# A Perceiver layer on one core: query shifts by DMA, masks and divisions of the causal part regrouped, projections in column groups

## The chip, the cores and the metric

The kernel runs on 1 core of one Trainium2 chip. The metric is the device time of one execution in microseconds; the median of three runs of the kernel before is 1228.5 us (1228.21 to 1228.61).

The engines have the profiler's names: PE (TensorE) multiplies matrices, and PEld is the loading of its stationary operand; DVE (VectorE), ACT (ScalarE) and POOL (GpSimd) do the elementwise work; SP (SyncE) issues most DMAs. ACT and POOL can issue DMAs too, each in its own queue of instructions.

## The reference

The input x has B=4 sequences of T=256 rows with D=256 columns, and a context has 4096 rows for each sequence. Three residual steps follow one another; LN is a layer norm without weights:

```python
x = x + cross_attention(LN(x), ctx)    # 16 heads of 16; softmax over 4096 keys
x = x + causal(LN(x))                  # linear attention with random features
x = x + ffn(LN(x))                     # w_down(silu(w_gate h) * (w_up h)), hidden 768
```

In the cross-attention, Q = LN(x) Wq + bq, K = ctx Wk + bk, V = ctx Wv + bv, scores are QK/4, and the result goes through Wh + bh.

In the causal part, q and k of each head (16 numbers) are normalised to length 1 and turned into 64 features, `exp(clip(q·omega*sqrt(2s) - s, -20, 20))` times a weight, for two values of s and 32 columns of omega each. With features F(q), F(k), row t of the result is the sum over t' ≤ t of (F(q_t)·F(k_t')) v_t', divided by the same sum without v, at least 1e-6; then Wout + bout.

The weights of the feed-forward are int32 and are multiplied by 1/127.

## The kernel before

**Cross-attention** is the main loop. A unit u is one sequence b and one quad q of four heads (16 units). Each unit takes NS=16 steps of 256 keys. Row groups of 32 partitions hold the four heads of a quad: 16 rows of a head's numbers, one row (the first, 32j) for a shift, the rest zero or one. kts are three buffers of keys in that form, with ones in row 32j; so what stands in row 32j of the query tile qa is added to every score. It holds minus the maximum of that query's scores over all keys, which makes the exp safe.

Therefore the maxima of a unit must be known before its scores begin. In step n the loop computes, beside the scores of step n, the maxima of step s = n + NS + LEAD, with LEAD = 2: two steps before a unit ends, all the maxima of the next are there. At this point (w = 14) `shift` (L719 to L733) makes qa for it.

What PE, ACT and DVE do in one iteration n, in the order of their queues (`manual_schedule`: the order in which the code issues the instructions is the order in each queue of PE, ACT, DVE and SP; POOL's instructions are not in it):
- for heads (0,1), then heads (2,3): pt, the scores in row groups (L745), with pm, products for the maxima of the other two heads (L708); ACT takes e = exp(pt) (L750); DVE reduces pm to mx (L715).
- half of a projection of the context, for a later pair of units (EARLY = 8): pk (L642), which ACT copies as ku with the bias (L650) and SP's DMAs then put into kts (L653); or pv (L672), which ACT copies into v (L679). Both are in column groups: four matmuls of 32 columns each, side by side.
- pav (L765), values of step n−1, also in column groups, added by DVE to av (L775).
- at w = 14, `shift`: DVE reduces mx to neg, negated (L722), which is a sparse tile [128 queries, 2, 4, 32] of which only one column in 32 is not zero; after the projection's copy on ACT, `turn` (L724 to L731) transposes it on PE into pn (L727, two of 128*128), and DVE adds qT (L731), which gives qa. The call of `shift` is ahead of the projection in the code, that of `turn` behind its copy.
- at fixed steps of the next unit, `finish`: transposes pt_x, division, a bias on POOL (L802), eight small DMAs on SP (xo<-on, L806), transposes px, and the projection py (L823).

PSUM is one pool of 8 banks, taken in turn: a new tile waits until the readers of the tile that had the bank eight allocations before are done.

**The causal part** begins in the last two units: `start_causal` (L286 to L367) fills places of missing projections with pieces. In them `queries_keys` (L207, pqk of L211) and `values` (L224, pv1 of L229) project LN(x) with full 128*128 matmuls.

**The tail** begins near 1070 us, with a loop over n = 0 to 16 (L513 to L566). n is a sequence and quad of the causal part. At each n: values (po, L430; ACT copies it to avT, L435) of n−1; scores (pa, L411 and L416) of n, in two parts of two heads, each head's `at` multiplied by a mask on DVE (L421); `divide` of n−1 (PE transposes pt_o L442, DVE den L444 and L445, att L446); features of a later quad for some n (pf L275, DVE clip L281, ACT exp L282, POOL fac L283); then pieces of `fills[n]`: casts of the weights (ACT, L394, `weight(i)`, a whole weight of 768 KB each), output projection (L453), and the feed-forward of sequences that are done (L469). A weight is loaded when the one before has been cast.

The mask is made once on POOL by affine_select (L375): ones, and zeros where the key comes after the query, in the first and third of three blocks; the second block (first keys, second queries) needs none.

Of the kernel before, what the change touches and what calls it, by code (L numbers as in the profile page):

```python
# [20 lines left out]
P = 128  # L21
# [18 lines left out]
def perceiver_layer(  # L40
# [96 lines left out]
    def normalised(z, tiles):  # L137
# [47 lines left out]
    def causal_in(b):  # L185

        tiles = (2 * b, 2 * b + 1)
        z = lnp.tile([P, 2, D], F32, tag="z1", name="z1", bufs=4)
        got = []

        def norm():
            normalised(lambda t: z[:, t % 2, :], tiles)
            for t in tiles:
                nc.gpsimd.tensor_tensor(xr[:, t, :], xr[:, t, :], rest[9], ALU.add)

        def turn():
# [6 lines left out]
            nc.vector.tensor_copy(zT.rearrange("p k (i t) -> p k i t", t=P), ps)  # L203

        sqs = {}

        def queries_keys(i):  # L207
            t, zT = tiles[i], got[0]
            ps = bank([P, 2 * D], "pqk")
            for k in range(KC):  # L210
                nc.tensor.matmul(  # L211
                    ps, lhsT=zT[:, k, i * P : (i + 1) * P], rhs=rest[3][:, k, : 2 * D],
                    start=k == 0, stop=k == KC - 1,
                )
            nc.vector.tensor_tensor(qk[t], ps, rest[4][:, : 2 * D], ALU.add)
            sqs[i] = lnp.tile([P, 2 * D], F32, tag="sq", name="sq")
            nc.gpsimd.tensor_tensor(sqs[i], qk[t], qk[t], ALU.mult)

        def squares(i):
            nc.vector.tensor_reduce(  # L220
                nrm[:, tiles[i], :], sqs[i].rearrange("p (h d) -> p h d", d=HD), AX.X, ALU.add
            )

        def values():  # L224
            zT = got[0]
            ps = bank([P, 2, D], "pv1")
            for i in range(2):
                for k in range(KC):
                    nc.tensor.matmul(  # L229
                        ps[:, i, :], lhsT=zT[:, k, i * P : (i + 1) * P], rhs=rest[3][:, k, 2 * D :],  # L230
                        start=k == 0, stop=k == KC - 1,
                    )
# [52 lines left out]
    def start_causal():  # L285
# [75 lines left out]
        return norms, [call(lambda pieces: [piece() for piece in pieces], pieces) for pieces in others]  # L361

    finish = cross_attention(
        tc, xr, load_x, load_rest, ctxT, wq_sb, bq_sb, wkP, bk_sb, wvP, eps, ident, layernorm, transposed,
        qT, kts, lnp, bank, rest, start_causal)
    wout_sb = rest[8]

# [19 lines left out]
    coming = []  # L387

    def weight_load(i):
        src = (w_gate, w_up, w_down)[i]  # L390
        coming.append(load(src, list(ws[i].shape), "w_i", mybir.dt.int32, nc.sync, late))

    def weight(i):
        nc.scalar.activation(ws[i], coming[i], AF.Copy, scale=(1.0, 0.5, 1.0)[i] / 127.0)  # L394
        if i + 1 < len(ws):
            weight_load(i + 1)

    def attend(n):


        b, q = divmod(n, NQ)
        ats, got = [], []

        def scores():
            for part in range(2):
# [12 lines left out]
                    )  # L418
                for pa in pas:
                    at = work.tile([P, 3, P], F32, tag="at", name="at", bufs=8)  # L420
                    nc.vector.tensor_tensor(at, pa, mask, ALU.mult)  # L421
                    ats.append(at)

        def values():
            po = bank([P, T], "po")
            for i in range(2):
                for j, at in enumerate(ats):
# [6 lines left out]
            oT = work.tile([P, T], F32, tag="avT", name="avT")  # L434
            nc.scalar.copy(oT, po)  # L435
            got.append(oT)

        def divide():
            oT = got.pop()
            pt = bank([P, 2, 4, 32], "pt_o")  # L440
            for i in range(2):
                nc.tensor.transpose(pt[:, i].rearrange("p j r -> p (j r)"), oT[:, i * P : (i + 1) * P], ident)  # L442
            den = work.tile([P, 2, 4], F32, tag="den", name="den")
            nc.vector.tensor_scalar(den, pt[:, :, :, HD], 1e-6, None, ALU.max)  # L444
            nc.vector.reciprocal(den, den)  # L445
            nc.vector.tensor_tensor(  # L446
                att[:, 2 * b : 2 * b + 2, 64 * q : 64 * q + 64].rearrange("p t (j d) -> p t j d", d=HD),
                pt[:, :, :, :HD], den.unsqueeze(3).to_broadcast([P, 2, 4, HD]), ALU.mult,
            )

        return scores, values, divide
# [61 lines left out]
    with tc.manual_schedule(engines={ET.PE, ET.Activation, ET.DVE, ET.SP}):  # L513
        normalise, turn15, project15 = finish
        normalise()
        weight_load(0)
# [3 lines left out]
        fills[1] += [lambda: weight(0)]  # L520
        fills[2] += [turn15, lambda: weight(1)]
        fills[3] += [project15, norm3, lambda: weight(2)]
# [45 lines left out]

def cross_attention(tc, xr, load_x, load_rest, ctxT, wq_sb, bq_sb, wkP, bk_sb, wvP, eps,
                    ident, layernorm, transposed, qT, kts, lnp, bank, rest, start_causal):  # L570

# [20 lines left out]
    with ExitStack() as st:  # L592
# [4 lines left out]

        vs = big.tile([P, NCH, KT, VP], F32, tag="v", name="v")

        negs = [big.tile([P, 2, 4, 32], F32, tag=f"neg{i}", name="neg") for i in range(2)]  # L600


        wk_sb = big.tile([P, KC, D], F32, tag="wk_sb", name="wk_sb")
# [26 lines left out]
        def key(p, c, queues=(nc.sync, nc.sync)):  # L630
# [5 lines left out]
            def half(part):  # L636
# [1 line left out]
                made.append(pk)  # L638
                cs = slice(part * (CH // 2), (part + 1) * (CH // 2))
                for k in range(KC):  # L640
                    for j in range(4):
                        nc.tensor.matmul(  # L642
                            pk[32 * j : 32 * j + 32, :],
                            lhsT=wk_sb[:, k, m * P + 32 * j : m * P + 32 * j + 32], rhs=x[:, k, cs],
                            start=k == 0, stop=k == KC - 1,
                        )

            def out(part):
                cs = slice(part * (CH // 2), (part + 1) * (CH // 2))
# [10 lines left out]
        def value(p, c):  # L660
# [4 lines left out]
            def half(part):  # L665
                pv = bank([P, 2, P], "pv")
                made.append(pv)
                for i in range(2):
                    t0 = (2 * part + i) * P
                    for k in range(KC):  # L670
                        for j in range(4):
                            nc.tensor.matmul(  # L672
                                pv[32 * j : 32 * j + 32, i, :], lhsT=x[:, k, t0 + 32 * j : t0 + 32 * j + 32],
                                rhs=wv_sb[:, k, m * P : (m + 1) * P], start=k == 0, stop=k == KC - 1,
                            )

            def out(part):
                to = vs[:, c, 2 * part : 2 * part + 2, : 8 * (HD + 1)]
# [38 lines left out]
            return products, reduce  # L717

        def shift(u):  # L719
            b, q = divmod(u, NQ)  # L720
            neg = negs[u % 2]
            nc.vector.tensor_reduce(neg[:, :, :, 0], mxs.pop(u), AX.X, ALU.max, negate=True)  # L722

            def turn():  # L724
                pn = bank([P, T], "pn")
                for i in range(2):
                    nc.tensor.transpose(  # L727
                        pn[:, i * P : (i + 1) * P], neg[:, i].rearrange("p j r -> p (j r)"), ident
                    )
                qas[u] = small.tile([P, T], F32, tag="qa", name="qa")  # L730
                nc.vector.tensor_tensor(qas[u], pn, qT[:, q, b * T : (b + 1) * T], ALU.add)  # L731

            return turn  # L733

# [42 lines left out]
        def finish(u):  # L777
# [41 lines left out]
            def project():  # L819
                t, oT = 2 * b + q // 2, rows_of.pop(b)  # L820
                py = bank([P, D], "py1")
                for k in range(KC):
                    nc.tensor.matmul(  # L823
                        py, lhsT=oT[:, k, :], rhs=rest[1][:, k, :], start=k == 0, stop=k == KC - 1
                    )
# [35 lines left out]
        with tc.manual_schedule(engines={ET.PE, ET.Activation, ET.DVE, ET.SP}):  # L861
# [33 lines left out]
            for neg in negs:  # L895
                nc.vector.memset(neg, 0.0)
            for piece in normal[1]:
                piece()
            whole(key(0, 2))
# [55 lines left out]
            for n in range(NU * NS + 1):  # L955
# [113 lines left out]
```

## Time and profile before

| | |
|---|---|
| median of three runs | 1228.5 us |
| the profiled execution's own time | 1229.02 us |
| its span | 1227.3 us |
| mean granted PE clock | 0.997 of full |
| DMA, mean over the span | 78 GB/s |
| PE over the 40 slices, in tenths | 7 in the first, 9 in the next 34, then 5, 9, 9, 9, 8 |

The span is cut into 40 slices of 30.7 us. PE's busy share is at 90% or more from the second slice to the 35th, between 50 and 60% in the 36th (1074 to 1105 us, the first stretch of the tail), and at 80% or more to the end. The main loop is thus the part from about 73 us, when unit 0's qa is there, to about 1068 us.

How much each kind of work costs, from the groups of instructions: busy time in us, mean of one in ns.

```profile
L715 DVE TENSOR_REDUCE mx<-pm 128x1 f32<-128x512 f32 x1024 | 635.6, 684 | 145.4 <-PE pm L708 145.3
L750 ACT ACTIVATE e<-pt 128x512 f32<-128x512 f32 x1024 | 529.2, 602 | 384.2 <-PE pm L708 359.6
L745 PE MATMUL pt<-qa,kt 32*128 32x256 f32 x4096 | 500.2, 388 | 1.3 <-DVE av L775 0.7
L708 PE MATMUL pm<-kt,qT 32*128 32x512 f32 x2048 | 494.6, 616 | 0.0
L765 PE MATMUL pav<-e,v 128*32 128x256 f32 x4096 | 269.8, 380 | 0.0
L672 PE MATMUL pv<-wv_sb,ctx 128*32 128x128 f32 x4096 | 137.5, 276 | 0.0
L642 PE MATMUL pk<-ctx,wk_sb 128*32 128x256 f32 x2048 | 136.7, 388 | 0.0
```

A line has: line of the program, engine, operation, output<-inputs, for PE the size of the stationary tile (32*128 is a row group of 32 partitions, 128*32 a column group), shapes, count; then busy time and mean; then the idle time of the engine just before such instructions and what ended most of it. Matmuls in different groups of the array overlap, so their means don't add up to PE's time.

### The profile page before, as it was taken

What the parts mean: (1) busy time and instruction counts of PE and PEld (TensorE: products, weight loads), DVE (VectorE), ACT (ScalarE), POOL (GpSimd) and SP (SyncE); (2) the same over time, 40 slices, a digit from 0 to 9 for tenths busy, and PEclk for the clock granted to TensorE, in tenths of its full rate; (3) what the DMA queues carried; (4) which work ended last, traced back from release to release, by engine and by line L of the source; (5) the groups of instructions that cost most, each with busy time, mean ns of one, the idle gap of its engine ahead of it and who ended that gap; (6) DMA issues with size and microseconds to landing.
All of it is one profiled execution on the core that took longest, in us unless ns stands there. A gap on an engine that the chain in (4) does not pass through costs nothing.

```text
span 1227.3 us, 42096 instructions
## 1 busy us (share of the span) xinstructions
PE 1193.0 (97%) x17712; PEld 807.0 (66%) x17712; DVE 927.9 (76%) x1823; ACT 673.0 (55%) x1394; POOL 60.2 (5%) x115
## 2 busy tenths in 40 slices
PE   7999999999999999999999999999999999959998
PEld 3566667666766676667666776677667755536777
DVE  6887777777777777777777777777788877577763
ACT  3456665566666655666656556655566546641311
POOL 4010000000000000000000000000001012120100
PEclk9999999999999999999999999999999999999999
DMA  6452331233123322332233213322232000020000
GB/s 208 135 192 67 101 114 56 80 105 106 64 79 89 116 71 63 103 119 72 60 102 106 86 58 91 103 90 73 86 105 91 5 1 4 2 80 1 10 9 18
DMA packets 57756, 95.78 MB, mean 78 GB/s; under 512 B 29024, under 2 KB 31712, under 8 KB 57568
## 3 DMA queue, kind: packets, MB, share of 16 engines
q1 hardware_dynamic: 56640, 92.44, 24.3%
q8 instruction: 140, 2.29, 0.8%
q10 hardware_dynamic: 416, 0.66, 0.2%
q14 instruction: 48, 0.39, 0.1%
q0 software_dynamic: 512, 0.00, 0.0%
HBM read 74.17 MB, written 1.05 MB: 61 GB/s over the span
## 4 chain that ended last, share of the span: by engine, by line
PE 92%; DVE 4%; ACT 1%; DMA 1%; issue 1%; SPq 0%; POOL 0%; DVEq 0%; ACTq 0%
PE pt L745 22%; PE pm L708 18%; PE pav L765 18%; PE pk L642 11%; PE pv L672 10%; PE pd L504 2%; PE pg L492 1%; PE pu L492 1%; PE pq L848 1%; PE pqk L211 1%; PE po L430 1%; PE pa L411 1%; PE py L823 1%; PE py L466 1%; DVE mx L715 1%; PE pf L275 1%
## 5 line engine op out<-in xcount | busy, mean ns | idle before, releaser
L715 DVE TENSOR_REDUCE mx<-pm 128x1 f32<-128x512 f32 x1024 | 635.6, 684 | 145.4 <-PE pm L708 145.3
L750 ACT ACTIVATE e<-pt 128x512 f32<-128x512 f32 x1024 | 529.2, 602 | 384.2 <-PE pm L708 359.6
L745 PE MATMUL pt<-qa,kt 32*128 32x256 f32 x4096 | 500.2, 388 | 1.3 <-DVE av L775 0.7
L708 PE MATMUL pm<-kt,qT 32*128 32x512 f32 x2048 | 494.6, 616 | 0.0
L745 PEld LDWEIGHTS pt<-qa,kt 32*128 32x128 f32 x4096 | 317.0, 184 | 117.2 <-ACT v L679 43.2
L765 PE MATMUL pav<-e,v 128*32 128x256 f32 x4096 | 269.8, 380 | 0.0
L708 PEld LDWEIGHTS pm<-kt,qT 32*128 32x128 f32 x2048 | 172.2, 184 | 15.5 <-issue 3.7
L765 PEld LDWEIGHTS pav<-e,v 128*32 128x32 f32 x4096 | 128.7, 110 | 73.9 <-ACT e L750 4.7
L775 DVE TENSOR_TENSOR av<-pav,av 128x256 f32<-128x256 f32 x240 | 101.7, 424 | 65.7 <-PE pav L765 65.4
L672 PE MATMUL pv<-wv_sb,ctx 128*32 128x128 f32 x4096 | 137.5, 276 | 0.0
L642 PE MATMUL pk<-ctx,wk_sb 128*32 128x256 f32 x2048 | 136.7, 388 | 0.0
L672 PEld LDWEIGHTS pv<-wv_sb,ctx 128*32 128x32 f32 x4096 | 104.2, 109 | 43.5 <-DVE mx L715 42.7
L642 PEld LDWEIGHTS pk<-ctx,wk_sb 128*32 128x32 f32 x2048 | 54.8, 110 | 67.1 <-DVE mx L715 39.0
L650 ACT ACTIVATE ku<-pk,bk_sb 128x256 f32<-128x256 f32 x128 | 63.2, 495 | 11.2 <-PE pk L642 9.9
L679 ACT COPY v<-pv 128x256 f32<-128x256 f32 x128 | 51.4, 402 | 9.9 <-PE pv L672 9.9
L802 POOL TENSOR_TENSOR on<-on,bv_sb 128x64 f32<-128x64 f32 x32 | 9.2, 308 | 820.5 <-DVE on L797 820.5
L421 DVE TENSOR_TENSOR at<-pa,mask 128x384 f32<-128x384 f32 x64 | 31.2, 550 | 7.0 <-PE pa L416 7.0
L282 ACT ACTIVATE kt<-kt,shift 128x512 f32<-128x512 f32 x32 | 22.4, 725 | 22.0 <-DVE kt L281 22.0
L281 DVE TENSOR_SCALAR kt<-pf,low,top 128x512 f32<-128x512 f32 x32 | 23.7, 803 | 3.9 <-PE pf L275 3.9
L492 PE MATMUL pg<-zT,wg 128*128 128x256 f32 x96 | 23.0, 382 | 0.7 <-ACT zT L484 0.7
L496 ACT ACTIVATE th<-pg 128x512 f32<-128x512 f32 x12 | 7.1, 594 | 29.8 <-PE pg L492 29.8
L492 PE MATMUL pu<-zT,wu 128*128 128x256 f32 x96 | 22.7, 379 | 0.0
(126 smaller groups left out, 565.6 us busy)
## 6 DMA issues: line engine op xcount, KB each, us to landing
ctx<-in_ctxT_dram SPq DMA_DIRECT2D x128, 512.0 KB
kt<-ku SPq DMA_DIRECT2D x508, 32.0 KB
xo<-on SPq DMA_DIRECT2D x128, 8.0 KB
xr<-in_x_dram SPq DMA_DIRECT2D x4, 256.0 KB
out_dram<-o SPq DMA_DIRECT2D x8, 128.0 KB
wqkv_sb<-in_wqkv_dram SPq DMA_DIRECT2D x1, 768.0 KB
w_i<-in_w_gate_dram SPq DMA_DIRECT2D x1, 768.0 KB
w_i<-in_w_up_dram SPq DMA_DIRECT2D x1, 768.0 KB
```

The costliest lines, as they stand in the source:

```text
L421: nc.vector.tensor_tensor(at, pa, mask, ALU.mult)
L492: nc.tensor.matmul(ps[:, i, :], lhsT=w[:, k, ns], rhs=zT[:, k, :], start=k == 0, stop=k == KC - 1)
L642: nc.tensor.matmul(pk[32 * j : 32 * j + 32, :], lhsT=wk_sb[:, k, m * P + 32 * j : m * P + 32 * j + 32], rhs=x[:, k, cs], start=k == 0, sto ...
L650: nc.scalar.activation(ku[:, cs], made.pop(), AF.Identity, bias=bk_sb[:, m : m + 1])
L672: nc.tensor.matmul(pv[32 * j : 32 * j + 32, i, :], lhsT=x[:, k, t0 + 32 * j : t0 + 32 * j + 32], rhs=wv_sb[:, k, m * P : (m + 1) * P], sta ...
L679: nc.scalar.copy(to.rearrange("p t (h d) -> p t h d", d=HD + 1)[:, :, :, :HD], made.pop().rearrange("p t (h d) -> p t h d", d=HD),)
L708: nc.tensor.matmul(pm, lhsT=qT[rows, q, t0 : t0 + P], rhs=kt[rows, c * CH : (c + 1) * CH], start=True, stop=True,)
L715: nc.vector.tensor_reduce(mx[:, i, j, c : c + 1], pm, AX.X, ALU.max)
L745: nc.tensor.matmul(pt[:, i, :], lhsT=kt[rows, ks], rhs=qa[rows, :], start=True, stop=True)
L750: nc.scalar.activation(e, pt, AF.Exp, scale=0.25)
L765: nc.tensor.matmul(pav[32 * h : 32 * h + 32, :], lhsT=v[:, t % KT, c0 : c0 + 32], rhs=es[n, h][:, i, :], start=i == 0, stop=i == 1,)
L775: nc.vector.tensor_tensor(avs[u], pav, avs[u], ALU.add)
```

## The change

1. *The shift's rows by DMA.* For all units but the first, `shift` no longer transposes. POOL copies the queries qT into qa, all rows. neg is now a dense tile [128 queries, 4 heads, 2], which DVE reduces as before. Then eight DMAs of 128 elements each put the maxima of head j and query half i into row 32j of qa: those of (j, i) = (0,0) and (2,0) are issued by ACT, the other six by POOL. In ACT's queue they come ahead of the projection's copy of the same iteration. `turn` is only called for unit 0.
2. *Masks.* In part 0 of the tail's scores, ACT copies pa to `at`, and POOL's affine_select zeroes what is masked, in blocks one and three of `at`, in one instruction. Part 1 still multiplies by the mask on DVE.
3. *Division* is done once for two quads, at even n, with four transposes into one bank, and one den and att for eight heads.
4. *Weights* are loaded and cast in six halves, one in each of n = 1 to 6, two loads ahead of the casts, instead of three whole ones in n = 1 to 3.
5. *Column groups.* pqk, pv1 and py1 (the projection of `finish`) are done as four matmuls of 32 columns each by a new `product4`; pk and pv call it too and stay what they were.

```diff
+    def product4(out, lhsT, rhs, **flags):
+        for j in range(4):
+            js = slice(32 * j, 32 * j + 32)
+            nc.tensor.matmul(out[js], lhsT=lhsT[:, js], rhs=rhs, **flags)
...
-                nc.tensor.matmul(
-                    ps, lhsT=zT[:, k, i * P : (i + 1) * P], rhs=rest[3][:, k, : 2 * D],
+                product4(
+                    ps, zT[:, k, i * P : (i + 1) * P], rest[3][:, k, : 2 * D],
                     start=k == 0, stop=k == KC - 1,
                 )
...
+    def weight_load(n):
+        i, half = divmod(n, 2)
+        w = ws[i].shape[1] // 2
+        src = (w_gate, w_up, w_down)[i][:, half * w : half * w + w, :]
+        coming[n] = work.tile([P, w, ws[i].shape[2]], I32, tag="w_i", name="w_i")
+        nc.sync.dma_start(out=coming[n], in_=src)
+    def weight(n):
...
+        nc.scalar.activation(
+            ws[i][:, half * w : half * w + w, :], coming.pop(n), AF.Copy, scale=(1.0, 0.5, 1.0)[i] / 127.0
+        )
+        if n + 2 < 6:
+            weight_load(n + 2)
...
-                    nc.vector.tensor_tensor(at, pa, mask, ALU.mult)
+                    if part == 0:
+                        nc.scalar.copy(at, pa)
+                        nc.gpsimd.affine_select(
+                            out=at[:, 0:3:2, :], in_=at[:, 0:3:2, :], compare_op=ALU.is_ge, fill=0.0, base=0,
+                            pattern=[[0, 2], [1, P]], channel_multiplier=-1,
+                        )
+                    else:
+                        nc.vector.tensor_tensor(at, pa, mask, ALU.mult)
...
-            if n > 0:
+            if n > 0 and n % 2 == 0:
                 steps[n - 1][2]()
...
         def shift(u):
             b, q = divmod(u, NQ)
-            neg = negs[u % 2]
-            nc.vector.tensor_reduce(neg[:, :, :, 0], mxs.pop(u), AX.X, ALU.max, negate=True)
+            qa = qas[u] = small.tile([P, T], F32, tag="qa", name="qa")
+            if u == 0:
+                nc.vector.tensor_reduce(neg0[:, :, :, 0], mxs.pop(u), AX.X, ALU.max, negate=True)
+            else:
+                neg = small.tile([P, 4, 2], F32, tag="neg", name="neg")
+                nc.vector.tensor_reduce(neg.rearrange("p j i -> p i j"), mxs.pop(u), AX.X, ALU.max, negate=True)
+                nc.gpsimd.tensor_copy(qa, qT[:, q, b * T : (b + 1) * T])
+                for j in range(4):
+                    for i in range(2):
+                        (nc.scalar if (j, i) in ((0, 0), (2, 0)) else nc.gpsimd).dma_start(
+                            out=qa[32 * j : 32 * j + 1, i * P : (i + 1) * P], in_=neg[:, j, i : i + 1]
+                        )
...
                 if w == NS - LEAD and u + 1 < NU:
-                    turn = shift(u + 1)
+                    shift(u + 1)
...
-                if w == NS - LEAD and u + 1 < NU:
-                    turn()
```

More of the change, by code (lines that the diff above doesn't have):

```diff
@@ L228, in values @@
                 for k in range(KC):
-                    nc.tensor.matmul(
-                        ps[:, i, :], lhsT=zT[:, k, i * P : (i + 1) * P], rhs=rest[3][:, k, 2 * D :],
+                    product4(
+                        ps[:, i, :], zT[:, k, i * P : (i + 1) * P], rest[3][:, k, 2 * D :],
                         start=k == 0, stop=k == KC - 1,
@@ L363, in perceiver_layer @@
     finish = cross_attention(
-        tc, xr, load_x, load_rest, ctxT, wq_sb, bq_sb, wkP, bk_sb, wvP, eps, ident, layernorm, transposed,
+        tc, xr, load_x, load_rest, ctxT, wq_sb, bq_sb, wkP, bk_sb, wvP, eps, ident, layernorm, transposed, product4,
         qT, kts, lnp, bank, rest, start_causal)
@@ L386, in perceiver_layer @@
     ]
[L387 to L396, printed above, removed]
+    coming = {}
+    def weight_load(n):
[5 more added lines that the diff above has]
+    def weight(n):
+        i, half = divmod(n, 2)
+        w = ws[i].shape[1] // 2
+        nc.scalar.activation(
[3 more added lines that the diff above has]
+            weight_load(n + 2)
+    got = []
     def attend(n):
         b, q = divmod(n, NQ)
-        ats, got = [], []
+        ats = []
         def scores():
@@ L433, in values @@
                     )
-            oT = work.tile([P, T], F32, tag="avT", name="avT")
+            oT = work.tile([P, T], F32, tag="avT", name="avT", bufs=3)
             nc.scalar.copy(oT, po)
@@ L438, in divide @@
         def divide():
[L439 to L443, printed above, removed]
+            pt = bank([P, 2, 8, 32], "pt_o")
+            for m, oT in enumerate(got):
+                for i in range(2):
+                    nc.tensor.transpose(
+                        pt[:, i, 4 * m : 4 * m + 4].rearrange("p j r -> p (j r)"), oT[:, i * P : (i + 1) * P], ident
+                    )
+            got.clear()
+            den = work.tile([P, 2, 8], F32, tag="den", name="den")
             nc.vector.tensor_scalar(den, pt[:, :, :, HD], 1e-6, None, ALU.max)
@@ L446, in divide @@
             nc.vector.tensor_tensor(
-                att[:, 2 * b : 2 * b + 2, 64 * q : 64 * q + 64].rearrange("p t (j d) -> p t j d", d=HD),
-                pt[:, :, :, :HD], den.unsqueeze(3).to_broadcast([P, 2, 4, HD]), ALU.mult,
+                att[:, 2 * b : 2 * b + 2, 64 * q - 64 : 64 * q + 64].rearrange("p t (j d) -> p t j d", d=HD),
+                pt[:, :, :, :HD], den.unsqueeze(3).to_broadcast([P, 2, 8, HD]), ALU.mult,
             )
@@ L515, in perceiver_layer @@
         normalise()
-        weight_load(0)
+        for n in range(2):
+            weight_load(n)
         NB = B * NQ
@@ L519, in perceiver_layer @@
         norm3, turn3, qk3, sq3, v3, _ = causal_in(3)
-        fills[1] += [lambda: weight(0)]
-        fills[2] += [turn15, lambda: weight(1)]
-        fills[3] += [project15, norm3, lambda: weight(2)]
+        for n in range(6):
+            fills[n + 1] += [lambda n=n: weight(n)]
+        fills[2] += [turn15]
+        fills[3] += [project15, norm3]
         fills[4] += [turn3, lambda: qk3(0)]
@@ L569, in cross_attention @@
 def cross_attention(tc, xr, load_x, load_rest, ctxT, wq_sb, bq_sb, wkP, bk_sb, wvP, eps,
-                    ident, layernorm, transposed, qT, kts, lnp, bank, rest, start_causal):
+                    ident, layernorm, transposed, product4, qT, kts, lnp, bank, rest, start_causal):
     nc = tc.nc
@@ L598, in cross_attention @@
         vs = big.tile([P, NCH, KT, VP], F32, tag="v", name="v")
-        negs = [big.tile([P, 2, 4, 32], F32, tag=f"neg{i}", name="neg") for i in range(2)]
+        neg0 = big.tile([P, 2, 4, 32], F32, tag="neg0", name="neg0")
         wk_sb = big.tile([P, KC, D], F32, tag="wk_sb", name="wk_sb")
@@ L640, in half @@
                 for k in range(KC):
[L641 to L646, printed above, removed]
+                    product4(
+                        pk, wk_sb[:, k, m * P : (m + 1) * P], x[:, k, cs], start=k == 0, stop=k == KC - 1
+                    )
             def out(part):
@@ L670, in half @@
                     for k in range(KC):
[L671 to L675, printed above, removed]
+                        product4(
+                            pv[:, i, :], x[:, k, t0 : t0 + P], wv_sb[:, k, m * P : (m + 1) * P],
+                            start=k == 0, stop=k == KC - 1,
+                        )
             def out(part):
@@ L720, in shift @@
             b, q = divmod(u, NQ)
-            neg = negs[u % 2]
-            nc.vector.tensor_reduce(neg[:, :, :, 0], mxs.pop(u), AX.X, ALU.max, negate=True)
+            qa = qas[u] = small.tile([P, T], F32, tag="qa", name="qa")
[6 more added lines that the diff above has]
+                for j in range(4):
+                    for i in range(2):
+                        (nc.scalar if (j, i) in ((0, 0), (2, 0)) else nc.gpsimd).dma_start(
+                            out=qa[32 * j : 32 * j + 1, i * P : (i + 1) * P], in_=neg[:, j, i : i + 1]
+                        )
             def turn():
@@ L727, in turn @@
                     nc.tensor.transpose(
-                        pn[:, i * P : (i + 1) * P], neg[:, i].rearrange("p j r -> p (j r)"), ident
+                        pn[:, i * P : (i + 1) * P], neg0[:, i].rearrange("p j r -> p (j r)"), ident
                     )
-                qas[u] = small.tile([P, T], F32, tag="qa", name="qa")
-                nc.vector.tensor_tensor(qas[u], pn, qT[:, q, b * T : (b + 1) * T], ALU.add)
+                nc.vector.tensor_tensor(qa, pn, qT[:, q, b * T : (b + 1) * T], ALU.add)
             return turn
@@ L822, in project @@
                 for k in range(KC):
-                    nc.tensor.matmul(
-                        py, lhsT=oT[:, k, :], rhs=rest[1][:, k, :], start=k == 0, stop=k == KC - 1
-                    )
+                    product4(py, oT[:, k, :], rest[1][:, k, :], start=k == 0, stop=k == KC - 1)
                 nc.vector.tensor_tensor(xr[:, t, :], py, xr[:, t, :], ALU.add)
@@ L894, in cross_attention @@
             nc.vector.memset(flat[:, :, 8 * (HD + 1) :], 1.0)
-            for neg in negs:
-                nc.vector.memset(neg, 0.0)
+            nc.vector.memset(neg0, 0.0)
             for piece in normal[1]:
```

## The prediction

> **What bounds the kernel now.** First the page's first and fourth parts, busy time by engine and the shares of the chain that ended last:
>
> ```profile
> PE 1193.0 (97%) x17712; PEld 807.0 (66%) x17712; DVE 927.9 (76%) x1823; ACT 673.0 (55%) x1394; POOL 60.2 (5%) x115
> PE 92%; DVE 4%; ACT 1%; DMA 1%; issue 1%; SPq 0%; POOL 0%; DVEq 0%; ACTq 0%
> ```
>
> TensorE is the bound, so work taken from it counts in full, and so does every wait that reaches it. Next the groups of instructions, for the lines that the change touches:
>
> ```profile
> L727 PE MATMUL pn<-ident,neg 128*128 128x128 f32 x32 | 6.6, 287 | 1.7 <-DVE neg L722 0.9
> L74 POOL DMA_DIRECT2D bk_sb<-in_bkP_dram x16 | 10.9, 689 | 1.9 <-DMA bk_sb<-in_bkP_dram 1.5 <-issue 0.3
> L375 POOL TENSOR_SCALAR_AFFINE_SELECT mask<-mask 128x128 f32<-128x128 f32 x2 | 0.5, 292 | 0.1
> L421 DVE TENSOR_TENSOR at<-pa,mask 128x384 f32<-128x384 f32 x64 | 31.2, 550 | 7.0 <-PE pa L416 7.0
> ```
>
> The third column is the idle time before the group and what ended it: masks wait for scores, not the reverse. Then the timeline of one shift (iteration 14 of a unit, in the steady loop), where the starts in the first column matter:
>
> ```profile
> 129.82 0.50 ACT L650 ACTIVATE ku<-pk,bk_sb 128x256 f32<-128x256 f32 x1
> 130.15 0.21 DVE L722 TENSOR_REDUCE neg<-mx 128x8 f32<-128x64 f32 x1
> 130.48 0.20 PEld L727 LDWEIGHTS pn<-ident,neg 128*128 128x128 f32 x2 [0.51 <-ACT ku L650]
> 130.85 0.19 PEld L745 LDWEIGHTS pt<-qa,kt 32*128 32x128 f32 x2 [0.17 <-issue]
> 131.60 0.41 PEld L708 LDWEIGHTS pm<-kt,qT 32*128 32x128 f32 x4
> 134.64 0.19 PEld L745 LDWEIGHTS pt<-qa,kt 32*128 32x128 f32 x2 [0.41 <-ACT ku L650]
> ```
>
> Iteration 15 starts at 130.85, the first of the new unit (16) at 134.64: the next reader of qa is 4.3 us behind the end of neg (130.36). Last the tail, from 1070 us: 35 us in which TensorE works 21.45, and 85 in which it works 82.95 (the window answer), with waits behind the weights' cast on ScalarE:
>
> ```profile
> 1082.03 1.48 ACT L394 ACTIVATE wg<-w_i 128x1536 f32<-128x1536 int32 x1 [5.04 <-DMA w_i<-in_w_gate_dram]
> 1083.82 0.69 PE L442 MATMUL pt_o<-ident,avT 128*128 128x128 f32 x2 [3.59 <-ACT avT L435]
> 1092.02 0.44 PE L442 MATMUL pt_o<-ident,avT 128*128 128x128 f32 x2 [2.57 <-ACT avT L435]
> 1104.03 3.68 PE L211 MATMUL pqk<-wqkv_sb,zT 128*128 128x512 f32 x4 [3.79 <-DVE zT L203]
> ```
>
> [...] from the last matmul of pav (column mode) to the first load of pt (row mode) 0.31 us pass, against 0.216 between matmuls within a mode. [...] The trace has only the start-up's transfers on that queue: 16 elements each, issues of 0.48 to 0.60 us where nothing disturbs them, landing 2.85 us after issue at best, 5.0 in the median. [...] one bk_sb issue took 3.27 us while DVE filled kt (L874). [...]
>
> **The change, part by part.** Against the profiled execution's own 1229.0 us (span 1227.3 and 1.7 around it); the median of the runs shown, 1228.5, is 0.5 lower.
>
> *Transposes gone.* A plain iteration of the loop takes 3.81 us, one with a shift 4.27: pn costs 0.46. Fifteen shifts lose it (unit 0 keeps its own): 15 x 0.46 = −6.9. The DVE add (0.42) goes too; DVE has slack there.
>
> *The shift's two DMAs on ScalarE.* They wait for neg, and queued behind them are ku or v of iteration 14, then the exps of 15; the first pm of iteration 15's second group takes that PSUM bank. neg ends at 130.36, 0.06 to the queue. The price of an issue on ScalarE is the start-up's: four kt transfers in a row took 2.50 us, and the next ACTIVATE came only after:
>
> ```profile
> 12.77 2.50 ACTq L653 DMA_DIRECT2D kt<-ku  x4
> 15.38 0.47 ACT L853 ACTIVATE qT<-pq,bq_sb 128x256 f32<-128x256 f32 x1 [2.64 <-DMA kt<-ku]
> ```
>
> I take 0.57 each for rows of 4-byte elements (bounds 0.33, SP's weights in the tail, and 1.01, below). ku then ends at 130.36 + 0.06 + 1.14 + 0.05 + 0.50 = 132.11, 0.05 more to TensorE: 132.16. Without pn that load is wanted at 131.60 − 0.46 = 131.14: a stall of 1.02, with v (0.40) 0.92; 0.97 on the mean. What was hidden behind pav no longer is.
>
> *The six on GpSimd.* The copy of qT waits for a reader one unit back and is done long before (0.48 us, hidden; behind neg it would add that much to each stall). The six DMAs start at 130.42 and issue one after another. The last is for head 3, whose pt is loaded 0.55 into the iteration: at 134.64 − 0.46 + 0.55 = 134.73 without any stall. It lands at 130.42 + 5t + d, t the issue and d issue to landing. No row shows 128 elements from GpSimd. SP shows 128 elements of 4 bytes twice:
>
> ```profile
> 71.47 1.01 SPq L51 DMA_DIRECT2D nod<-in_nodes_dram  x1
> 72.53 0.65 SPq L51 DMA_DIRECT2D wei<-in_weights_dram  x1
> ```
>
> Bounds: t from 0.48 (16 elements, GpSimd) to 1.01; d from 2.0 (kt<-ku in the loop, SP, by semaphore[...]) to 5.0 (bk_sb's median, when the queues were full of the first loads). I take t = 0.65, because eight times the elements can hardly cost what 16 do, and d = 2.85, the best that this queue shows: 130.42 + 3.25 + 2.85 = 136.52, which is 1.79 after the need. ScalarE's 0.97 lies inside this, since both stall the same engine one after the other. 15 x 1.79 = +26.9. Ends: at t = 0.48, d = 2.0 the rows are there at 134.82 and only ScalarE's 14 x 0.97 = 13.6 is left (at n=238 no projection follows); at d = 5.0 the stall is 3.94, +59; at t = 1.01, 3.59, +54. It can't be below nothing: no engine gets work earlier by it.
>
> *Column groups.* py as four 128*128 matmuls takes 1.06 us, pk of the same size in column groups 0.87: −0.19, seven in the loop: −1.3. pqk (1.95) and pv1 (1.92) by the same rhythm 4 x 0.432 = 1.73 each: in the loop −2.3, in the tail −0.3. Sum −3.9. Bounds 0 (no faster than one wide matmul) and −6 (a mode switch of 0.3 saved at some).
>
> *Tail.* Halved weights: a cast is 0.74 instead of 1.48, and its first half's transfer lands sooner, so avT waits some 1.55 less at 1082. No division after quad 3: the pt_o at 1092.02 and its 2.57 go, of which 2.3 before py. Together −3.85. Part 0's two masks (0.97 of the 1.94 for four) leave DVE for ScalarE copies (about 0.48, between the 0.35 of 256 columns and the 0.60 of 512) and GpSimd selects (two of 0.292 in one, about 0.5). In the DVE stretch 1097.9 to 1104.0, which ends in pqk's wait of 3.79, at and den leave: −2.7; quad 4's masks −0.72 (0.97 less 0.25 for a larger den), quad 8's −0.7, five merged pt_o pairs at 0.15 −0.75, +0.15 at the end where values now wait for the slower of two routes. Sum −8.6, all before 1126 us; after that TensorE hardly waits, so nothing is gained there. If ScalarE's copies queue behind exps and avT, the masks' part (4.1) is gone and up to as much is lost.
>
> *Sum.* −6.9 + 26.9 − 3.9 − 8.6 = +7.5: 1236.5 own, 1236.0 as the median.
>
> **Rivals.**
> - *The rows land in time* (faster). Everything hangs on the GpSimd chain. If 5t + d is at most 5.28 (t = 0.49 with d = 2.85, or t = 0.65 with d = 2.0), only ScalarE's stall stays: −6.9 + 13.6 − 12.5 = −5.8, 1222.7. For it: [...] landings of 2.0 us in the loop. Against: 0.48 is the price for 16 elements. It is faster than before as long as the stall is under 19.4 / 15 = 1.29 per shift, that is 5t + d under 5.6.
> - *In time, and ScalarE's issue is short* (0.33): the stall falls to about 0.5, −12.4: 1216. Against: four measured issues of about 0.6.
> - *The landing is as late as at the start* (d = 5.0) or t is 1.0: 1263 to 1268. Against: those queues were full then; at a shift the sixteen engines are lightly used.
> - *The tail gives nothing*, the ScalarE and GpSimd route taking the masks' place on the way to po: 8.6 more than the forecast, 1244.6, or with rows in time 1231. For it: ScalarE is what TensorE waits for at 1083 and 1092. Against: half a cast is in the way instead of a whole one.
>
> **How the numbers follow.** Forecast 50% (stalls of 1.4 to 3.2: 1230 to 1257); in time 25%; in time and short 8%; very late 7%; tail without gain 10%. About 0.2% is what a measurement of this kernel can tell from no change. Slower by more: the forecast but for its low edge (45), very late (7), most of the last (7): 59%. Faster: 33%. Within: 8%. The range leaves out half of the very late and the lowest of the short: 1216 to 1262. Faster and slower both have weight; the forecast's own range is 1230 to 1257.
>
> **What would show it.** An iteration 15 with a pm load that waits about 1 us for ScalarE's ku or v; an iteration 16 whose pt loads wait for a DMA into qa, about 0.8 more; GpSimd DMA records of 0.65 us; the shift's two iterations together 1.3 us longer than before; py, pqk and pv1 at 0.87 and 1.73; 35 us from 1070 shortened by about 8. Wrong would be: issues of 0.5 or a landing of 2 us (then faster), a GpSimd DMA stretched by DVE, or waits of po for at in the tail.

## The result and the profile after

The kernel after takes 1237.33 us (median of 1236.18 to 1238.58) against 1228.55 us before: a ratio of 1.0072, 95% interval 1.0055 to 1.0090, so 8.8 us slower. The prediction was 1236.0, within 1216 to 1262, with slower the likeliest side.

The page of the kernel after, busy time and the chain that ended last, and the groups of the new instructions (POOL's DMAs of the shift, the masks that DVE keeps), with the line of these DMAs in the list of issues (median us from issue to landing at the end):

```profile
PE 1201.5 (97%) x17970; PEld 798.3 (65%) x17970; DVE 907.2 (73%) x1751; ACT 689.1 (56%) x1429; POOL 126.7 (10%) x252
...
PE 84%; issue 5%; DVE 5%; ACT 2%; DMA 2%; SPq 1%; POOL 1%; DVEq 0%; POOLq 0%; ACTq 0%
...
L755 POOL DMA_DIRECT2D qa<-neg x90 | 48.1, 541 | 597.5 <-DVE neg L751 499.8
...
L444 DVE TENSOR_TENSOR at<-pa,mask 128x384 f32<-128x384 f32 x32 | 16.3, 551 | 15.5 <-PE pa L432 15.4
...
qa<-neg POOLq DMA_DIRECT2D x90, 0.5 KB, 2.3
```

TensorE's share of the chain fell from 92% to 84%, and that of issues rose from 1% to 5%. These shares say where the chain ran, not how much was lost: 8% of the span would be 99 us, and the kernel is 8.8 us slower. An issue of GpSimd costs 0.541 us.

Where the time went is read best from the periods of the main loop's iterations, each from its first pt to the next one's, after minus before. They differ in the shift's three iterations and in those with a piece in column groups:

| us, after minus before | sum |
|---|---|
| iteration 14 of the fourteen shifts in the loop: transposes gone | −6.5 |
| the fifteenth, at n = 238: transposes gone, and a piece in column groups (−0.2) | −0.6 |
| iteration 15: TensorE waits for ScalarE's ku or v | +14.0 |
| iteration 16: pt waits for the rows | +11.8 |
| the other pieces in column groups, all the rest of the loop | −3.0 |
| before the loop | +0.2 |
| the tail, from the last unit's last iteration on | −7.7 |
| together (spans 1235.5 and 1227.3) | +8.2 |

A shift beside a key projection in the timeline of the kernel after. Where the prediction's lines had pn, two DMAs of ScalarE and six of GpSimd now follow neg:

```profile
130.36 0.21 DVE L751 TENSOR_REDUCE neg<-mx 128x8 f32<-128x64 f32 x1
...
130.65 1.35 ACTq L755 DMA_DIRECT2D qa<-neg  x2
...
131.16 3.24 POOL L755 DMA_DIRECT2D qa<-neg  x6 [49.48 <-issue]
...
131.79 0.53 SPq L651 DMA_DIRECT2D ctx<-in_ctxT_dram  x1
...
132.28 0.47 ACT L675 ACTIVATE ku<-pk,bk_sb 128x256 f32<-128x256 f32 x1 [2.11 <-DMA kt<-ku]
...
132.80 0.19 PEld L732 LDWEIGHTS pm<-kt,qT 32*128 32x128 f32 x2 [1.05 <-ACT ku L675]
...
135.72 0.29 PEld L779 LDWEIGHTS pt<-qa,kt 32*128 32x128 f32 x2 [0.41 <-issue]
...
137.09 0.45 PE L779 MATMUL pt<-qa,kt 32*128 32x256 f32 x1 [0.67 <-DMA qa<-neg]
```

Both waits are there: pm's load for the ku that stands behind ScalarE's DMAs (the releaser named at ku is an older DMA; ScalarE's own two issues fill 1.35 of the 2.11 us), and the new unit's pt for qa. And there is an instruction that the prediction did not reckon with: at 131.79, in the middle of GpSimd's six, SP issues a context load of 512 KB. A shift beside a value projection shows the contrast:

```profile
195.20 0.21 DVE L751 TENSOR_REDUCE neg<-mx 128x8 f32<-128x64 f32 x1
...
195.49 1.13 ACTq L755 DMA_DIRECT2D qa<-neg  x2
...
195.95 3.21 POOL L755 DMA_DIRECT2D qa<-neg  x6 [44.87 <-issue]
...
197.08 0.19 PEld L732 LDWEIGHTS pm<-kt,qT 32*128 32x128 f32 x2 [0.48 <-ACT v L703]
...
199.28 0.33 SPq L651 DMA_DIRECT2D ctx<-in_ctxT_dram  x1
```

Here the load leaves 3.87 us after the end of neg, when GpSimd has issued all. The packet records of GpSimd's queue say the same: beside value projections the last row packet ends 4.53 us after neg in five shifts of seven (4.8 in two); beside key projections 5.3 to 6.7. The waits of TensorE, as the growth of its iterations against the kernel before, in us per shift:

| mean per shift | beside keys, iteration 15 | 16 | beside values, iteration 15 | 16 |
|---|---|---|---|---|
| kernel after | 1.21 | 1.39 | 0.78 | 0.29 |

### The profile page after: what moved, and what is told of

Same layout as the page of the kernel before. It is cut to its first block, busy times and chain, and to the rows that moved or that the text cites. A ratio compares the mean times of both kernels' runs of the same rounds, so it can differ in the third digit from the quotient of the medians.

```text
span 1235.5 us, 42811 instructions
## 1 busy us (share of the span) xinstructions
PE 1201.5 (97%) x17970; PEld 798.3 (65%) x17970; DVE 907.2 (73%) x1751; ACT 689.1 (56%) x1429; POOL 126.7 (10%) x252
## 4 chain that ended last, share of the span: by engine, by line
PE 84%; issue 5%; DVE 5%; ACT 2%; DMA 2%; SPq 1%; POOL 1%; DVEq 0%; POOLq 0%; ACTq 0%
PE pt L779 20%; PE pm L732 17%; PE pav L799 16%; PE pv L159 10%; PE pk L159 9%; PE pd L530 2%; PE pg L518 1%; PE pu L518 1%; PE pq L880 1%; PE pqk L159 1%; PE pa L427 1%; SPq L678 1%; DMA kt<-ku 1%; DVE mx L739 1%; PE po L453 1%
## 5 line engine op out<-in xcount | busy, mean ns | idle before, releaser
L779 PE MATMUL pt<-qa,kt 32*128 32x256 f32 x4096 | 511.0, 389 | 3.8 <-ACT e L784 0.9
L732 PE MATMUL pm<-kt,qT 32*128 32x512 f32 x2048 | 501.4, 618 | 4.2 <-ACT ku L675 3.6
L755 POOL DMA_DIRECT2D qa<-neg x90 | 48.1, 541 | 597.5 <-DVE neg L751 499.8
L444 DVE TENSOR_TENSOR at<-pa,mask 128x384 f32<-128x384 f32 x32 | 16.3, 551 | 15.5 <-PE pa L432 15.4
```

The source lines that it names most:

```text
L732: nc.tensor.matmul(pm, lhsT=qT[rows, q, t0 : t0 + P], rhs=kt[rows, c * CH : (c + 1) * CH], start=True, stop=True,)
L755: (nc.scalar if (j, i) in ((0, 0), (2, 0)) else nc.gpsimd).dma_start(out=qa[32 * j : 32 * j + 1, i * P : (i + 1) * P], in_=neg[:, j, i : i ...
L779: nc.tensor.matmul(pt[:, i, :], lhsT=kt[rows, ks], rhs=qa[rows, :], start=True, stop=True)
```

## The experiments

The theory after the result (A): the shift by DMA costs more than the transposes it saves, by two waits, one for ScalarE's queue order and one for rows that a context load delays; column groups and tail gain. The rivals: (B) the loss sits in column groups or tail, (C) ScalarE's stall and the rows' lateness add up independently, (D) GpSimd's chain of issues is late by itself.

**The shift alone.** The kernel before with after's `shift`, nothing else:

```diff
-            neg = negs[u % 2]
-            nc.vector.tensor_reduce(neg[:, :, :, 0], mxs.pop(u), AX.X, ALU.max, negate=True)
+                nc.gpsimd.tensor_copy(qa, qT[:, q, b * T : (b + 1) * T])
+                for j in range(4):
+                    for i in range(2):
+                        (nc.scalar if (j, i) in ((0, 0), (2, 0)) else nc.gpsimd).dma_start(
...
-                if w == NS - LEAD and u + 1 < NU:
-                    turn()
```

> The kernel before with the shift's rows by DMA alone. Theory A (the shift costs, the rest gains): from the periods of iterations in the trace of the kernel after, 15 transposes gone are -7.0, the waits for ScalarE's copy in iteration 15 are +14.0 and the waits for rows in iteration 16 are +11.8, so 1228.5 + 18.8 = 1247 (1245 to 1249). Rival B (the loss sits in the column groups or in the tail's longer route, and the shift by DMA is about even): 1226 to 1231.

Measured 1247.18, ratio 1.0156 (1.0142 to 1.0170). **All but the shift.** The kernel after with the transposes kept, the same edit the other way round:

> The kernel after with the shift of before (transposes on TensorE), all else kept. Theory A: 1237.3 less 18.8, about 1218 (1216 to 1221): column groups -3.1 and the tail -7.7 against before. Rival B: 1235 or more.

Measured 1217.87, ratio 0.9915 (0.9901 to 0.9928). So B falls: the shift costs 18.6 to 19.5 us, everything else gains 10.7.

**ScalarE's DMAs behind the copy.**

```diff
                 if i < len(items) - NCH:
                     item[1](half)
+                if w == NS - LEAD and u + 1 < NU:
+                    rows()    # nc.scalar.dma_start for (0, 0) and (2, 0)
```

> The kernel after with ScalarE's two DMAs put behind the projection's copy in its queue; nothing else differs. Theory A, as the prediction has it (ScalarE's stall lies inside the wait for the rows): in the seven shifts beside key projections the stall only moves from iteration 15 to 16, in the seven beside value projections the 0.78 us fall to about 0.35, so 1237.3 - 3 = 1234 (1231 to 1236). Rival C (the two stalls add up): all of ScalarE's 14.0 goes, 1223.

Measured 1256.74, ratio 1.0237 (1.0217 to 1.0257): 19 slower than the kernel after, where one theory said 3 faster and the other 14. Both fall. Iteration 15's wait is gone in nearly every shift, as both had it (mean 0.08 us), but iteration 16 is 3.7 us longer beside keys and 3.3 beside values than in the kernel before. The timeline of this kernel beside a value projection:

```profile
196.36 0.21 DVE L751 TENSOR_REDUCE neg<-mx 128x8 f32<-128x64 f32 x1
...
197.11 3.22 POOL L756 DMA_DIRECT2D qa<-neg  x6 [44.87 <-issue]
...
199.67 0.33 SPq L651 DMA_DIRECT2D ctx<-in_ctxT_dram  x1
```

The context load now leaves 3.1 us after neg's end instead of 3.87: its buffer is released by iteration 15's projection on TensorE, which no longer stalls (in both kernels the load leaves 0.06 us after the end of pv: 199.61 and 199.67 here, 199.22 and 199.28 in the kernel after). The load meets the last rows, whose packets end 6.1 to 7.0 us after neg instead of 4.53. ScalarE's stall had kept the load away. A second loss follows the waits. In the windows of a shift beside keys (columns: time, busy time of PE, PEld, DVE, ACT and POOL with counts, granted clock, DMA share, GB/s):

```profile
134.00:137.60 3.60, 0.51 (x2) 0.11 (x1) 0.38 (x1) 0.00 (x0) 0.26 (x1) 0.95 0.26 67
137.60:141.60 4.00, 3.91 (x34) 3.33 (x38) 1.79 (x3) 1.42 (x3) 0.00 (x0) 0.61 0.21 51
```

After a wait of 3.2 us TensorE is granted a clock of 0.61 over 4 us, and that shift loses 5.4 us for a wait of 3.2. It is not the only one. In the profiled execution the clock is 0.5 for 3.41 us at six of the fourteen shifts and for 6.83 us at two; these eight lose 3.6 to 5.4 us in iteration 16, the six others 2.2 to 2.9. The kernel after has no such stretch in its loop.

So most of the 19 us is the slower clock, and less of it the later rows. The stretches last 34 us together and cost about 17 of them (an estimate: half), where the span grew by 25 against the kernel after's. This execution took 1262.24, the slowest of the five. In the median one the mean clock is 0.987 against 0.997, which by the same estimate is 12 to 13 of the 19 us.

**The same without context loads.** To see whether the load is the cause, this kernel leaves out the main loop's loads (all projections read the first four tiles):

```diff
-            for _, p, c in itertools.islice(loads, 1):
+            for _, p, c in itertools.islice(loads, len(contexts) < 4):
...
-            return contexts.pop(0)
+            contexts.append(contexts.pop(0))
+            return contexts[-1]
```

> The kernel with ScalarE's two DMAs behind the copy (the run before this one that came out at 1257), with the context loads of the main loop left out: after the first four, all projections read the same four tiles, so the result is another and only the time counts. Theory A (the stall of ScalarE had held TensorE back, and with it the release of a context buffer; without it the next context load of 512 KB goes out 3.1 us after the end of neg instead of 3.9, onto the last rows): waits in iteration 16 fall from 2.2 to 5.4 us to under 0.5, about 1216 (1211 to 1222). Rival (the rows are late by GpSimd's own chain once nothing else stalls): 1245 to 1257.

Measured 1222.43, ratio 0.9951 (0.9938 to 0.9965), 34 less than with the loads, and no stretch of the loop is at the slower clock. That the load makes rows late is shown. The time lies a hair above the range expected, because iteration 16 still waits 0.56 us in most shifts: what GpSimd's chain costs with nothing in its way, and what ScalarE's stall of 0.8 to 1.2 covers in the kernel after.

**The load out of the way.** The kernel after, with the load ahead of the key DMAs in SP's queue (and so one load more before the loop):

```diff
         def context(p, c):
-            load_context()
             return contexts.pop(0)
...
             def out(part):
+                if part == 1:
+                    load_context()
```

> The kernel after with each context load issued by SP ahead of the eight key DMAs of the item that frees its buffer instead of behind them; the same loads. Theory A (rows are late beside key projections because a context load of 512 KB, held up behind the key DMAs, is issued 1.2 to 2.3 us after the end of neg and shares the sixteen DMA engines with the rows): the seven waits of 0.85 to 2.3 us in iteration 16 go, -9.7, so about 1227.6 (1225 to 1231). Rival D (GpSimd's chain of six issues is late by itself): 1235 to 1238.

Measured 1228.91, ratio 1.0005 (0.9997 to 1.0013): 8.4 faster than the kernel after. Its shift beside keys, in the timeline:

```profile
131.26 0.21 DVE L754 TENSOR_REDUCE neg<-mx 128x8 f32<-128x64 f32 x1
...
132.07 3.26 POOL L758 DMA_DIRECT2D qa<-neg  x6 [45.78 <-issue]
...
133.70 0.19 PEld L735 LDWEIGHTS pm<-kt,qT 32*128 32x128 f32 x2 [1.04 <-ACT ku L676]
...
135.89 0.33 SPq L651 DMA_DIRECT2D ctx<-in_ctxT_dram  x1
...
136.62 0.48 PE L782 MATMUL pt<-qa,kt 32*128 32x256 f32 x2
```

The load leaves 4.4 us after neg, and pt starts unhindered 5.15 us after neg: waits in iteration 16 beside keys fell from 1.39 to 0.01 us, those in iteration 15 stayed (1.22). D falls for the kernel after: six issues of 0.54 are not late as long as ScalarE's stall stands ahead of them.

**More time for the rows.** LEAD = 3 brings the shift one iteration earlier:

```diff
-    LEAD = 2
+    LEAD = 3
...
-            extra = {10: 0, 13: 1}
+            extra = {10: 0, 12: 1, 14: 2}
```

> The kernel after with LEAD = 3: maxima run three steps ahead, so the shift comes one iteration (3.8 us) earlier and the rows have that much more time; ScalarE's DMAs stay ahead of the copy. Theory A: waits for rows gone (-11.8), waits for ScalarE's copy stay (14 of about 1.0): 1225.5 (1223 to 1228). Rival (the waits for rows only move, because the context load meets them elsewhere): 1232 to 1238.

Measured 1225.49, ratio 0.9975 (0.9965 to 0.9985). **Both waits taken away**, this and ScalarE's DMAs behind the copy:

> LEAD = 3 and ScalarE's two DMAs behind the projection's copy, else the kernel after. Theory A: both waits gone, so the transposes are saved for nothing: 1228.5 - 7.0 - 3.1 - 7.7 = 1210.7 (1208 to 1214), 7 under the kernel with the transposes kept. Rival (exps of the next iteration now stand behind ScalarE's DMAs and stall TensorE instead): 1218 to 1225.

Measured 1212.17, ratio 0.9869 (0.9854 to 0.9884), the fastest of all, 1.3% faster than before and 5.7 us faster than the kernel that keeps the transposes. The chain of its page:

```profile
PE 92%; DVE 6%; ACT 1%; DMA 1%; issue 0%; DVEq 0%; ACTq 0%
```

TensorE's share is back at 92%. No wait for rows or for the copy is left in its periods (mean 0.01 us); the transposes' 0.46 us per shift are saved. LEAD = 3 with the transposes kept was not run; by the traces the third step itself is about even: against the kernel with the transposes kept, it is 1.1 us more before the loop and 1.3 less in the loop's other iterations.

The waits per shift in one table, each from one profiled execution: "copy" is the growth of the iteration in which TensorE waits for the projection's copy, "rows" that of iteration 16. The rows "behind the copy" hold the time lost to the slower clock too, and so does one shift of "before with the shift alone" (4.15 us).

| mean per shift, us | copy, beside keys | rows, beside keys | copy, beside values | rows, beside values |
|---|---|---|---|---|
| after | 1.21 | 1.39 | 0.78 | 0.29 |
| before with the shift alone | 1.12 | 1.79 | 0.78 | 0.21 |
| load ahead | 1.22 | 0.01 | 0.77 | 0.25 |
| behind the copy | 0.07 | 3.74 | 0.10 | 3.33 |
| behind the copy, no loads | 0.05 | 0.91 | 0.03 | 0.62 |
| LEAD = 3 | 1.13 | 0.00 | 0.77 | 0.00 |
| LEAD = 3, behind the copy | 0.00 | 0.01 | 0.00 | 0.00 |

**Column groups alone**, the kernel before with pqk, pv1 and py1 by `product4`:

> The kernel before with pqk, pv1 and py1 in column groups alone. Theory A (four matmuls side by side take the time that pk's rhythm shows, and no mode is switched more often): -3.1 to -3.9, 1225. Rival (the narrower matmuls gain nothing, their four times as many weight loads cost it): 1228 to 1231.

Measured 1225.54, ratio 0.9978 (0.9970 to 0.9987): −2.6. Each py piece takes 0.197 less in its iteration, seven times.

**The tail's parts**, each alone in the kernel before. Halves of the weights:

> The kernel before with the integer weights loaded and cast in six halves alone. Theory A (avT waits behind a cast of 1.48 us in ScalarE's queue, and TensorE behind avT): -1.6 at the first cast, and up to 0.7 at the other two, so 1225.3 to 1226.9. Rival (TensorE waits for DVE anyway): 1228.

Measured 1225.62, ratio 0.9980 (0.9972 to 0.9988): −2.5. Division for two quads:

> The kernel before with the division done once for two quads alone. Theory A, the prediction's: the pt_o behind quad 3 goes with its wait (-2.3) and five merged pairs give 0.15 each: -3.0, 1225.5. Rival (the wait is taken over by the next reader of the same avT or of DVE): 1227.5 to 1228.5.

Measured 1228.21, ratio 1.0000 (0.9992 to 1.0009): nothing. Its timeline says where the gain went:

```profile
1096.13 1.48 ACT L394 ACTIVATE wd<-w_i 128x1536 f32<-128x1536 int32 x1 [3.83 <-DMA w_i<-in_w_down_dram]
...
1097.93 0.44 PE L444 MATMUL pt_o<-ident,avT 128*128 128x128 f32 x2 [3.11 <-ACT avT L437]
```

and the same pt_o in the kernel before:

```profile
1097.67 0.44 PE L442 MATMUL pt_o<-ident,avT 128*128 128x128 f32 x2 [2.06 <-DVE z L151]
```

The pt_o behind quad 3 is gone with its wait of 2.57, but the next one, whose avT stands behind the next whole cast, waits 3.11 instead of 2.06, and the last wait on DVE's zT is still ahead. Masks:

> The kernel before with the masks of part 0 by ScalarE's copy and GpSimd's select alone. Theory A, the prediction's: masks leave DVE's stretch, -4.1, 1224.4. Rival (the new route ends later than DVE's did: the trace of the kernel after shows po waiting 2.4 and 1.2 us for at from GpSimd): 1227 to 1231.

Measured 1226.43, ratio 0.9985 (0.9979 to 0.9992): −1.7 from the medians, between the two. The fastest kernel with the masks back on DVE:

```diff
-                    if part == 0:
-                        nc.scalar.copy(at, pa)
-                        nc.gpsimd.affine_select(
...
-                    else:
-                        nc.vector.tensor_tensor(at, pa, mask, ALU.mult)
+                    nc.vector.tensor_tensor(at, pa, mask, ALU.mult)
```

> The fastest so far (LEAD = 3, ScalarE's DMAs behind the copy; 1212.2) with all masks on DVE again. Theory A: 4 slower, 1216. Rival (ScalarE's and GpSimd's route gave nothing beside halves and pairs): 1210 to 1212.5.

Measured 1215.43, ratio 0.9895 (0.9882 to 0.9909): 3.3 slower than with after's masks. So the parts are worth more together than alone: masks 3.3 beside halves and pairs, halves 2.5 alone, which leaves 7.7 − 3.3 − 2.5 = 1.9 for the pairs once the casts are short. That is an estimate: halves and pairs together were run only at LEAD = 3, where the trace's tail is 5.3 us shorter than before's without the masks and 7.4 with them.

## Why the prediction was right, and what in it was not

- *Transposes*: −6.9 forecast, −6.9 measured (−6.5 and, at n = 238, −0.4).
- *ScalarE's two DMAs*: a stall of 1.02 beside keys and 0.92 beside values, 0.97 on the mean; measured 1.21, 0.78 and 1.00. The mechanism is the one forecast (load of pm, bank of ku or v, two issues ahead of it), and putting them behind the copy took it away. The issue was priced at 0.57; the records show 0.48 to 0.55 for the first and 0.61 to 0.89 for the second.
- *Six DMAs on GpSimd*: 0.82 us beyond ScalarE's stall, in every shift; measured 0.84 on the mean of fourteen. The size is right by luck, as the step behind it was not. The last issue was to begin 3.31 us after neg (0.06 + 5 x 0.65) and to land 2.85 later. It began at 3.22 (the first only at 0.56, t then 0.53), and where nothing was in the way it landed 1.9 us after that (its packets ended after 1.3). That eight times the elements can hardly cost what 16 do was an estimate, and wrong: an issue took 0.54 against 0.48. The longest of the ninety took 0.59, so none was stretched like the one of 3.27 at the start. By these numbers the rows of all shifts are in time behind ScalarE's stall, and beside values most are. What delays them beside keys is the context load, queued behind eight key DMAs on SP. The prediction held the DMA engines full at the start and "lightly used" at a shift. In the trace of the kernel before their busy share is 0.85 over the first 15 us; in the 5 us after neg it is 0.39 to 0.43 beside keys and 0.07 to 0.12 beside values. It priced this queue's transfers from the loaded start and so hit the mean with the wrong owner: seven shifts wait 1.39 on the mean and seven 0.29, where all were to wait 0.82.
- *The rival "in time"* is what the kernel after would be with the load elsewhere. That kernel came out at 1228.9, not at the rival's 1222.7: the rows still wait 1.8 in all, mostly beside values; column groups and the rest of the loop gain 1.6 less than forecast (in part by 3.4 us at a granted clock of 0.5 near the loop's end); the load brought forward costs 1.1 before the loop; ScalarE's stall is 0.3 more. These 4.8 us are the whole difference between the spans. The other 1.4 lie between executions: this kernel's profiled one was 0.9 under its median, that of the kernel before 0.5 over.
- *The fifteenth shift* was to wait 1.79 for rows; it does not wait at all.
- *Column groups*: −3.9 forecast, −2.6 by itself and −3.2 in the loop of the trace (−0.2 of it at n = 238). py's −0.19 is measured at −0.197; the rest is the pqk and pv1 pieces, forecast from pk's rhythm, of which part was lost.
- *Tail*: −8.6 forecast, −7.7 measured. Halves and pairs were given 4.6 (3.85 and five merged pairs at 0.15) and take 4.4; masks were given 4.1 and take 3.3. The waits of TensorE in the tail of the kernel after:

```profile
PE pqk L159 <- DVE zT L209: 4.0, 1, 4.0
...
PE po L453 <- POOL at L439: 3.6, 2, 2.4
```

The second line (total, times, longest) is the rival "the tail gives nothing" in small: in two places po waits for GpSimd's select, where exps and avT stand ahead of the copy on ScalarE. The wait of pqk for zT, from which I took 2.7 off, is as long as before (4.0 against 3.79), since what was gained came ahead of it.

The sum: +7.5 forecast, +8.2 between the two profiled spans, +8.8 between the medians.

What stays open: three shifts beside values (n = 30, 94 and 190) wait 0.6 to 0.9 us for rows though no context load is near. Their row packets end at 4.54 to 4.84 us after neg, hardly late, but the landing is told only at 5.67 to 6.20 instead of 5.10 to 5.14. In just these three of the seven, a fetch of instructions (a packet of 16 KB that takes 0.9 to 1.4 us) begins 2.6 to 3.9 us after neg. The same holds in other traces: over the shifts beside values of this kernel, of the shift alone and of the load ahead, and all fourteen of the kernel without loads, the twelve with a fetch in that stretch land at 5.39 us or later, the 23 without one by 5.26. No run took the fetches away, so the cause is likely and not shown.

## What to carry to other kernels

A DMA in the queue of an engine that also computes costs its issue there (0.5 to 0.9 us on ScalarE here), and everything behind it in that queue waits: put it behind what others wait for, or give it so much lead that nobody waits. Ask of a small, urgent transfer which large one may be released beside it, and what releases that: here a stall on one engine was what held a 512 KB load off the rows, and taking the stall away alone made the kernel 19 us slower, more than half of it, by the estimate above, through the slower clock that followed the waits. When two waits share a path, take both away at once before judging the idea: the shift by DMA costs 19 us as written and gains 6 with one more iteration of lead and two DMAs moved.

## What the runs showed of the hardware that was not expected

- Rows of 128 elements of 4 bytes cost GpSimd 0.54 us per issue, little over the 0.48 of 16 elements at the start. The first of a series begins 0.56 us after the instruction that releases it ends, ScalarE's 0.08.
- The rows came later beside a large load: those whose packets end 4.53 us after neg without one end at 5.3 to 7.0 when a 512 KB load is issued 1.2 to 3.1 us after it.
- TensorE lost more than its wait: the granted clock was 0.61 in the 4 us after a wait of 3.2, and a pm pair that takes 0.70 us at the start of an iteration took 1.31 there. With ScalarE's DMAs behind the copy, eight of fourteen shifts had a clock of 0.5 for 3.41 or 6.83 us. In seven of the eight the longest idle time of TensorE in the trace was 1.2 to 1.7 us. Six other shifts with 0.7 to 1.5 us kept the full clock, so the length of the wait alone does not decide; what does was not shown.
